# A two-layer attention and feed-forward kernel: the tails of its batches turn their rows on VectorE and through DRAM, and overlap

## The chip, the cores and the metric

The kernel runs on one core of a Trainium2 chip. The core has a matrix engine (TensorE, PE in the profile), VectorE (DVE), ScalarE (ACT), GpSimd (POOL) and SyncE (SP), each with its own instruction queue, and 16 DMA engines. Engines work side by side and wait for each other by semaphores; each runs its own instructions strictly in program order. In this kernel SP does nothing but issue DMAs. The metric is the device time of one execution in microseconds; lower is better. Times before the change are the median of three runs.

## The reference

There are 16 batches (B) of 256 tokens (S) by 256 features (D), in f32. Cut to what matters:

```python
x = x + L0_xattn(ctx, layernorm(x))   # 8 heads of 128; keys from ctx and x together, 512 per query
x = x + L0_ffn(layernorm(x))          # W1, W2 256 x 1024, each plus products of a batch's own tokens; gelu
x = x + L1_xattn(layernorm(x), ctx)   # "second attention": one head of 256, 256 keys
x = x + L1_ffn(layernorm(x))          # 8 experts, routing weights, silu(gate) * up, down
```

## The kernel before

**Layout.** A batch's tokens lie in two chunks (TC = 2) of 128 rows. A matrix product needs the summed index on the partitions, so rows must be turned between stages. Two ways of turning are in use. `transposed` (L269) has TensorE turn four 128x128 blocks into one PSUM bank (`turned`, L87); ScalarE or VectorE then copies it out. A *hop* is the other way: `to_blocks` (L279) lets VectorE turn 32x32 blocks into a tile, and SP writes that to DRAM; `from_blocks` (L293) has SP fetch it back in four DMAs, one for each block row, after which `in_order` only names the pieces in the right order. Hops already turn the inputs of batches 1 to 15, in `inputs`; the first attention's probabilities use the same scheme in `s2` (L820 on).

**Two kinds of work.** The main loop goes over n = 8 * batch + head. A *head step* emits, in this order: `s1(n)` (scores `sc`, row maxima, exponentials), `s1_scale`, `s0q(n+1)` (`pq`), `s0k(n+1)` (`pk`), filling work (`bulk`: `pv`, and units of `inputs`), `s3(n-2)` (`po`, whose result VectorE puts into outT), `s2(n)` (probabilities through DRAM). A place to slip in other work, `gap()`, follows s1, s0q, s0k, each of the two calls of bulk, and s3; I number them 1 to 6. bulk has no `pv` at heads 0 and 1, one at heads 2 to 5 and two at heads 6 and 7. A unit of `inputs(b+1)` comes at heads 0 to 4, in bulk's first call, just after place 3: at head 1 it turns `cin` and `cn` on VectorE and writes them out, at heads 2 and 3 it fetches.

What is slipped in are *chains*, one for each batch. `chain(b)` is a generator which is made at head 2 of batch b+1 and does everything after the first attention: output projection `px` into x, layernorm, turned `ybT`, the batch's own weights (`ev`: two small writes and one 1 MB broadcast read on SP; `od`, `W1e`, `W2e`), `v1`, first feed-forward `ph`, gelu, second `pf`, layernorm `yc`, turned `ycT`, `pq1` (in the trace pq<-ycT,M), scores `sc1`, exponentials `pr`, turned `prT`, `po1` (po<-v,pT), layernorm `row`, turned `ydT`, the routing product `pl`. `route(b)` then works out slots and scatters rows. At the end experts are run over gathered rows, in groups; they fill the same places from the last heads on.

**What sets the order.** Everything is emitted by a planner at build time. `Clock.pe` adds up what TensorE is thought to take: 1.667 ns for a column of f32, at least 0.38 us. A `yield t` in a generator makes it due t us of that clock later. `gap()` runs the first job of `line` that is due until at least 0.8 us of TensorE work has been emitted; older chains stand first. The order that comes out is the program order of all engines' queues. SP's too: a DMA that must wait for its data holds up all DMAs emitted after it.

In a steady batch of the kernel before, chain b starts with px at head 2; y is applied after the last unit of the chain before (`behind.done`), in head 3; ph runs in heads 5 and 6, gelu in head 7 or later, pf up to place 3 of the next batch's head 0, yc at place 1 of head 1, pq1 at place 6, sc1 at place 1 of head 2, po1 at place 4 of head 2, row in head 2, pl at place 3 of head 3.

Of the kernel before, what the change touches and what calls it, by code (L numbers as in the profile page):

```python
# [29 lines left out]
def xattn_ffn_kernel(  # L30
# [37 lines left out]
    def mm_tile(n, name):  # L68
        return psum.tile([P, n], F32, tag="mm", bufs=5, name=name, padded_shape=[P, 512])

    def tr_tile(name):
        return psum.tile([P, 4, P], F32, tag="tr", bufs=1, name=name)

# [191 lines left out]

    def tr_mm_tile(name):
        return mm_tile(4 * P, name).rearrange("p (a t) -> p a t", t=P)

    def transposed(src, name, tile_=tr_tile):  # L269

        t = tile_(name)
        for d in range(DC):
            for c in range(TC):
                turned(t[:, d * TC + c, :], src[:, c, ts(d, P)], ident)
        return t.rearrange("p (d c) t -> p d (c t)", d=DC)
# [47 lines left out]
    def chain(b, A, behind):  # L323
# [8 lines left out]
        def mv_tile(tag):  # L332
            return small.tile([P, TC, 2], F32, tag=f"mv{tag}", bufs=2, name=f"mv_{tag}_{b}")

        mv = mv_tile("b")
        for c in range(TC):
            px = mm_tile(D, f"px_{b}_{c}")
            for h in range(H):
                mm(px, outT[:, h, ts(c, P)], A.Wo[:, h, :], start=(h == 0), stop=(h == H - 1))
                if h == H // 2 - 1:  # L340
                    yield
            nc.vector.tensor_tensor(x_b[:, c, :], px, x_b[:, c, :], ALU.add)
            stats(c, "b", mv)
            if c < TC - 1:
                yield
# [7 lines left out]
        yield 2.5  # L353
        while behind is not None and not behind.done:
            yield 0.4
# [15 lines left out]
        plus_row(x_b, lasting["b2"])  # L371
        yield 2.2
        tp = transposed(y, f"ybT_{b}")
        yT = wk.tile([P, DC, S], F32, tag="yT", name=f"ybT_{b}")
        nc.scalar.copy(yT, tp)
        yield


        v1 = wk.tile([P, TC, D], F32, tag="v1", name=f"v1_{b}")
        for m in range(TC):  # L380
            pv = mm_tile(D, f"pv1_{b}_{m}")
            for d in range(DC):
                mm(pv, cT[:, d, ts(m, P)], WvT[:, d, :], start=(d == 0), stop=(d == DC - 1))
            nc.scalar.copy(v1[:, m, :], pv)
            yield
        yield landed - Clock.pe

        od = wk.tile([P, DC, 2 * NI], F32, tag="od", name=f"od_{b}")
        nc.vector.tensor_scalar(od, yT[:, :, 2 : 2 + 4 * NI : 2], lasting["scale"], None, ALU.mult)
        W1e = wk.tile([P, DC, NI, D], F32, tag="W1e", name=f"W1e_{b}")  # L390
# [29 lines left out]
        for k in range(HC):  # L420
            ph = mm_tile(S, f"ph_{b}_{k}")
            for d in range(DC):
                mm(
                    ph, W1e[:, d].rearrange("p i a -> p (i a)")[:, ts(k, P)], yT[:, d, :],
                    start=(d == 0), stop=(d == DC - 1),
                )
            nc.vector.tensor_scalar(hT[:, k, :], ph, col("b1", k), None, ALU.add)  # L427
            if k % 2 == 1:
                i = k // 2
                if i + 2 < NI:  # L430
                    w1_rows(i + 2)
                if i + 1 < NI:
                    w2_block(i + 1)
                yield 1.0
                w2_add(i)

        done = []
# [13 lines left out]
        for c in range(TC):  # L451
# [7 lines left out]
            if c < TC - 1:  # L459
                yield  # L460


        rs = ln_rstd(mv, "q")
        yield 2.5
        y = wk.tile([P, TC, D], F32, tag="y", name=f"yc_{b}")
        ln_apply(y, x_b, mv, rs)

        plus_row(x_b, lasting["bv1"])
        yield 1.4
        tp = transposed(y, f"ycT_{b}")  # L470
        yT = wk.tile([P, DC, S], F32, tag="yT", name=f"ycT_{b}")
        nc.scalar.copy(yT, tp)
        rc = small.tile([P, TC], F32, tag="rc", bufs=2, name=f"rc_{b}")
        for c in range(TC):
            junk = wk.tile([P, D], F32, tag="pr1", bufs=2, name=f"junk_{b}_{c}")
            nc.vector.tensor_tensor_reduce(
                out=junk, in0=y[:, c, :], in1=g1, op0=ALU.mult, op1=ALU.add,
                scale=1.0, scalar=g0, accum_out=rc[:, c : c + 1],
            )
        yield 1.6  # L480
        q1T = wk.tile([P, DC, S], F32, tag="q1T", name=f"q1T_{b}")
        for m in range(DC):
            pq = mm_tile(S, f"pq1_{b}_{m}")
            for d in range(DC):
                mm(pq, M1[:, d, ts(m, P)], yT[:, d, :], start=(d == 0), stop=(d == DC - 1))
            nc.scalar.activation(q1T[:, m, :], pq, AF.Identity, bias=u1[:, m : m + 1], scale=QS1)
        yield 1.6
        probs = []
        for c in range(TC):
            sc = mm_tile(S, f"sc1_{b}_{c}")  # L490
            for m in range(DC):
                mm(sc, q1T[:, m, ts(c, P)], cT[:, m, :], start=(m == 0), stop=(m == DC - 1))

            nm = small.tile([P, 1], F32, tag="nm1", name=f"nm1_{b}_{c}")
            nc.vector.tensor_reduce(nm, sc, AX.X, ALU.max)
            nc.vector.tensor_tensor(nm, nm, rc[:, c : c + 1], ALU.add)
            nc.vector.tensor_tensor(nm, rc[:, c : c + 1], nm, ALU.subtract)
            pr = wk.tile([P, S], F32, tag="pr1", bufs=2, name=f"pr1_{b}_{c}")
            sm = small.tile([P, 1], F32, tag="sm1", name=f"sm1_{b}_{c}")
            nc.scalar.activation(pr, sc, AF.Exp, bias=nm, accum_out=sm)  # L500
            probs.append((pr, sm))
        yield 3.5
        tp = tr_tile(f"prT1_{b}")
        for c in range(TC):
            for m in range(TC):
                turned(tp[:, c * TC + m, :], probs[c][0][:, ts(m, P)], ident)
        pT = wk.tile([P, TC * TC, P], F32, tag="pT1", bufs=1, name=f"pT1_{b}")
        nc.vector.tensor_copy(pT, tp)
        yield 1.6
        mv = mv_tile("d")  # L510
        for c in range(TC):
            ri = small.tile([P, 1], F32, tag="ri1", name=f"ri1_{b}_{c}")
            nc.vector.reciprocal(ri, probs[c][1])
            po = mm_tile(D, f"po1_{b}_{c}")
            for m in range(TC):
                mm(po, pT[:, c * TC + m, :], v1[:, m, :], start=(m == 0), stop=(m == TC - 1))
            nc.vector.scalar_tensor_tensor(
                x_b[:, c, :], po, ri, x_b[:, c, :], ALU.mult, ALU.add
            )
            stats(c, "d", mv)  # L520
# [9 lines left out]
        nc.vector.tensor_copy(row[:, :, D + E], number[:, b * TC : (b + 1) * TC])  # L530
        yield 1.4
        tp = transposed(row, f"ydT_{b}")
        ydT = wk.tile([P, DC, S], F32, tag="yT", name=f"ydT_{b}")
        nc.scalar.copy(ydT, tp)
        yield 1.6
# [115 lines left out]
    class A:  # L651
        xs, ctxT, outT, cin, kvT, v = {}, {}, {}, {}, {}, {}
        row, z = {}, {}
        projected = set()

# [3 lines left out]
    with ExitStack() as sa, ExitStack() as sf:  # L659
# [18 lines left out]
        def inputs(b):  # L678
# [32 lines left out]
            if b == 0:  # L711
                for src, at_, beta, gamma in ((cn, 0, "bm", "gm"), (xn, S, "bl", "gl")):
                    tp = transposed(src, f"{src.name}_T", tr_mm_tile)
                    for d in range(DC):
                        scaled(tp[:, d, :], d, at_, beta, gamma)
                    yield
                tp = transposed(cin, f"cinT_{b}", tr_mm_tile)
                nc.vector.tensor_copy(A.ctxT[b], tp)
                return
# [117 lines left out]
        def s3(n):  # L837

            b, h = divmod(n, H)
            pT, v = heads.pop(n), A.v[b, h // HG]  # L840
            if h == 0:
                A.outT[b] = wh.tile([P, H, S], F32, tag="outT", name=f"outT_{b}")
            po = mm_tile(S, f"po_{b}_{h}")
            for j in range(JC):
                mm(
                    po, v[:, j, ts(h % HG, DH)],
                    pT.rearrange("p a c f -> p c a f")[:, :, :, ts(j, QB)],
                    start=(j == 0), stop=(j == JC - 1),
                )

            nc.vector.tensor_scalar(A.outT[b][:, h, :], po, col("bv", h), None, ALU.add)  # L851

# [5 lines left out]
        def turn(W, nat, Wt, rchunks, cchunks):  # L858
# [3 lines left out]
            for k in range(0, len(blocks), 4):  # L862
                tp = tr_mm_tile(f"turn_{W.name}_{k}")
                for n, (c, r) in enumerate(blocks[k : k + 4]):
# [11 lines left out]
        def fold(nq, nk):  # L876
# [9 lines left out]
            for d in range(DC):  # L886
                for m in range(DC):
# [3 lines left out]
                    )  # L891
            bkr = wk.tile([P, DC, P], F32, tag="pr1", bufs=2, name="bk_rep")
            for m in range(DC):
# [386 lines left out]
```

## Time and profile before

| | |
|---|---|
| median of three runs | 1898.36 us (1895.84 to 1899.13) |
| the profiled execution's own time | 1899.3 us, span 1897.6 us |
| TensorE busy | 1845.4 us, 97% of the span |
| VectorE, ScalarE, GpSimd busy | 1179.6, 594.8, 872.3 us |
| one batch in the steady part | 93.15 us |
| DMA busy in the steady part | 0.47 of 16 engines |
| mean granted TensorE clock | 0.991 |

A timeline row of the profile gives start and length in us, engine (q: its sequencer, for DMA issues), source line, operation, out<-in, shape and count; what stands in brackets is the idle time before it and what ended it. One f32 product appears as two matmul instructions. A waits row reads: who waited, for what, us in total, times, longest. A row of windows gives the stretch, its length, then busy us (and instructions) of PE, its weight loads, DVE, ACT and POOL, then the granted clock, DMA share and GB/s.

### The profile page before, as it was taken

The numbers are of one execution on the slowest core, as the hardware profiler recorded it, in microseconds if no ns is written. First come the engines' busy times: TensorE is split into PE (matmuls) and PEld (weight loads), VectorE is DVE, ScalarE is ACT, GpSimd is POOL, SyncE is SP. The second block draws the span as 40 slices with busy tenths as digits, with TensorE's granted clock in tenths as the row PEclk, the third lists the DMA queues.
The fourth block names the chain that finished last, engine by engine and source line by source line (L and its number), as shares of the span: only waits on it lengthen the run. The fifth ranks groups of instructions, "written<-read, shape, count | busy, mean of one in ns | idle before, by whom it ended". The sixth has DMA issues, their size and how long they took to land.

```text
span 1897.6 us, 22669 instructions
## 1 busy us (share of the span) xinstructions
PE 1845.4 (97%) x6822; PEld 1252.6 (66%) x6822; DVE 1179.6 (62%) x3211; ACT 594.8 (31%) x1309; POOL 872.3 (46%) x996
## 2 busy tenths in 40 slices
PE   8999999999999999999999999999999999999995
PEld 4566666666666666666666666667676767665554
DVE  5356667666666666666675766666657476656553
ACT  3333434343333333333333333333333221111110
POOL 3122353535353535353534444444434367766565
PEclk9999999999999999999999999999999999999998
DMA  6553445454545444444454444444435477999995
GB/s 217 160 170 103 161 137 159 141 166 138 162 140 159 148 151 157 151 147 149 146 160 151 149 154 143 159 140 160 142 118 177 135 200 194 250 234 241 249 220 96
DMA packets 235083, 309.89 MB, mean 163 GB/s; under 512 B 27036, under 2 KB 195912, under 8 KB 232904
## 3 DMA queue, kind: packets, MB, share of 16 engines
q1 hardware_dynamic: 204184, 256.80, 43.2%
q0 software_dynamic: 30720, 51.54, 11.5%
q8 instruction: 57, 0.93, 0.2%
q14 instruction: 74, 0.61, 0.1%
q10 hardware_dynamic: 48, 0.01, 0.0%
HBM read 157.51 MB, written 150.73 MB: 162 GB/s over the span
## 4 chain that ended last, share of the span: by engine, by line
PE 90%; DVE 3%; DMA 2%; ACT 2%; POOL 1%; issue 1%; SPq 1%; ACTq 0%; POOLq 0%; DVEq 0%
PE po L83 13%; PE pv L83 13%; PE sc L83 12%; PE pk L83 10%; PE pq L83 7%; PE px L83 6%; PE pf L83 6%; PE ph L83 5%; PE pg L83 5%; PE pu L83 5%; PE pd L83 5%; ACT pr L810 1%; DMA wx<-in_L_ffn_Wg_dram 1%; DVE tb L827 1%; POOL out_dram L1123 1%
## 5 line engine op out<-in xcount | busy, mean ns | idle before, releaser
L818 POOL TENSOR_SCALAR pr<-pr,ri 128x512 f32<-128x512 f32 x256 | 183.9, 726 | 478.9 <-DVE ri L817 477.4
L810 ACT ACTIVATE pr<-sc,nm 128x512 f32<-128x512 f32 x256 | 173.8, 683 | 506.2 <-DVE nm L804 505.8
L638 POOL DMA_INDIRECT slots_d<-row,at_slot x256 | 268.7, 1050 | 121.6 <-DVE at_slot L634 64.8
L1123 POOL DMA_INDIRECT out_dram<-o,at x128 | 200.0, 1562 | 128.7 <-DMA out_dram<-o,at 37.8
L83 PE MATMUL po<-pT,v 128*128 128x256 f32 x1024 | 246.9, 385 | 8.9 <-DMA pT<-hop 8.9
L83 PE MATMUL sc<-kT,qT 128*128 128x512 f32 x512 | 241.5, 594 | 0.9 <-ACT kT L743 0.9
L83 PE MATMUL pk<-kvT,Wk_sb 128*128 128x512 f32 x512 | 240.7, 592 | 0.0
L83 PE MATMUL pv<-Wv_sb,kvT 128*128 128x512 f32 x512 | 238.6, 595 | 0.0
L83 PEld LDWEIGHTS po<-pT,v 128*128 128x128 f32 x1024 | 194.2, 192 | 63.2 <-issue 28.4
L804 DVE TENSOR_REDUCE nm<-sc 128x1 f32<-128x512 f32 x256 | 162.1, 666 | 16.9 <-PE sc L83 16.9
L827 DVE STREAM_TRANSPOSE tb<-pr 128x512 f32<-128x512 f32 x256 | 165.3, 683 | 7.2 <-DMA hop<-tb 7.2
L851 DVE TENSOR_SCALAR outT<-po,cvec 128x256 f32<-128x256 f32 x128 | 60.8, 475 | 164.3 <-PE po L83 164.3
L83 PEld LDWEIGHTS pv<-Wv_sb,kvT 128*128 128x128 f32 x512 | 96.0, 190 | 95.1 <-issue 89.2
L83 PEld LDWEIGHTS sc<-kT,qT 128*128 128x128 f32 x512 | 97.5, 191 | 69.4 <-issue 61.5
L83 PEld LDWEIGHTS pk<-kvT,Wk_sb 128*128 128x128 f32 x512 | 97.5, 190 | 68.0 <-issue 61.2
L1098 ACT ACTIVATE sg<-pg 128x384 f32<-128x384 f32 (+3 forms) x82 | 41.3, 504 | 312.3 <-PE pg L83 299.3
L83 PE MATMUL pg<-yTd,wx 128*128 128x384 f32 (+3 forms) x328 | 127.6, 512 | 11.2 <-DMA wx<-in_L_ffn_Wg_dram 7.0
L83 PE MATMUL pq<-kvT,Wq_sb 128*128 128x256 f32 x512 | 132.5, 381 | 0.0
L83 PE MATMUL pu<-yTd,wx 128*128 128x384 f32 (+3 forms) x328 | 125.3, 505 | 0.3 <-DVE hT L427 0.2
L83 PE MATMUL pd<-wx,hTd 128*128 128x256 f32 x512 | 123.8, 379 | 0.2 <-DVE hTd L1109 0.2
L83 PE MATMUL ph<-ybT,W1e 128*128 128x256 f32 x512 | 121.4, 380 | 0.1
L83 PEld LDWEIGHTS pq<-kvT,Wq_sb 128*128 128x128 f32 x512 | 96.6, 191 | 36.7 <-issue 22.7
(197 smaller groups left out, 2685.9 us busy)
## 6 DMA issues: line engine op xcount, KB each, us to landing
hop<-tb SPq DMA_DIRECT2D x128, 512.0 KB
pT<-hop SPq DMA_DIRECT2D x512, 128.0 KB
ev<-ev_d SPq DMA_DIRECT2D x16, 1024.0 KB
rows<-slots_d SPq DMA_DIRECT2D x31, 397.5 KB
hop_rows_b<-rows_b SPq DMA_DIRECT2D x29, 384.0 KB
yTd<-hop_rows_b SPq DMA_DIRECT2D x116, 96.0 KB
rows<-slots_d SPq DMA_DIRECT2D x8, 530.0 KB
cin<-in_ctx_dram SPq DMA_DIRECT2D x16, 256.0 KB
```

Of the source, the lines that this page charges most:

```text
L83: nc.tensor.matmul(out, lhsT, rhs, **kw)
L638: ins = nc.gpsimd.indirect_dma_start(out=slots_d[part], out_offset=bass.IndirectOffsetOnAxis(ap=at_slot[:, c, e : e + 1], axis=0), in_=row ...
L804: nc.vector.tensor_reduce(nm, sc, AX.X, ALU.max, negate=True)
L810: nc.scalar.activation(pr, sc, AF.Exp, bias=nm, accum_out=sm)
L818: nc.gpsimd.tensor_scalar(pr, pr, ri, 1.0, ALU.mult, ALU.mult)
L827: nc.vector.transpose(tb[:, :, c, :], heads[n][c][0].rearrange("p (m f) -> p m f", m=QP))
L851: nc.vector.tensor_scalar(A.outT[b][:, h, :], po, col("bv", h), None, ALU.add)
L1098: nc.scalar.activation(self.sg, self.pg, AF.Tanh, scale=0.5)
L1123: ins = nc.gpsimd.indirect_dma_start(out=out_rows[0 : sum(NTOKS[: self.part + 1]), :], out_offset=bass.IndirectOffsetOnAxis(ap=self.at[:, ...
```

## The change

All four turned tiles of a chain take hops: after each of yb, yc, pr and row, `to_blocks` is emitted at once, `from_blocks` 3.6 us of planner time later, and a use 4.0 later (for yb the 15 us until `ev` is thought to land). yT of the first feed-forward and of pq1 are read in place; pT and ydT are first copied by ScalarE. v1 moves from before ph to between yc's fetch and pq1. The wait for the whole chain in front goes: yb waits until ph of the chain in front is emitted (`fed`), od until its pf is (`fed_forward`), and only yc waits for its end. outT becomes twelve tiles of one head each instead of two of eight heads. PSUM: the bank for turning joins the pool of mm tiles, six instead of five.

```diff
-        return psum.tile([P, n], F32, tag="mm", bufs=5, ...)
-    def tr_tile(name):
-        return psum.tile([P, 4, P], F32, tag="tr", bufs=1, name=name)
+        return psum.tile([P, n], F32, tag="mm", bufs=6, ...)
...
+        def raw_tile(tag, name):
+            return wk.tile([P, QP, DC, TC, QB], F32, tag=tag, name=name)
...
-        while behind is not None and not behind.done:
+        while behind is not None and b - 1 not in A.fed:
             yield 0.4
         y = wk.tile([P, TC, D], F32, tag="y", name=f"yb_{b}")
...
         plus_row(x_b, lasting["b2"])
-        yield 2.2
-        tp = transposed(y, f"ybT_{b}")
-        yT = wk.tile([P, DC, S], F32, tag="yT", name=f"ybT_{b}")
-        nc.scalar.copy(yT, tp)
-        yield
-        v1 = ...   # moved
+        hop = to_blocks(wk, y, TC, "tbc", 1, f"yb_{b}_b")
+        yield 3.6
+        yTb = raw_tile("yT", f"ybT_{b}")
+        from_blocks(yTb, hop)
+        yT = in_order(yTb)
         yield landed - Clock.pe
+        while behind is not None and b - 1 not in A.fed_forward:
+            yield 0.4
...
         rs = ln_rstd(mv, "q")
         yield 2.5
+        while behind is not None and not behind.done:
+            yield 0.4
         y = wk.tile([P, TC, D], F32, tag="y", name=f"yc_{b}")
         ln_apply(y, x_b, mv, rs)
         plus_row(x_b, lasting["bv1"])
-        yield 1.4
-        tp = transposed(y, f"ycT_{b}")
-        yT = wk.tile([P, DC, S], F32, tag="yT", name=f"ycT_{b}")
-        nc.scalar.copy(yT, tp)
+        hop = to_blocks(wk, y, TC, "tbc", 1, f"yc_{b}_b")
...
-        yield 1.6
+        yield 3.6
+        yTc = raw_tile("raw_c", f"ycT_{b}")
+        from_blocks(yTc, hop)
+        landed = Clock.pe + 4.0
+        v1 = ...   # a yield after each of its two products
+        yield landed - Clock.pe
...
-        yield 3.5
-        tp = tr_tile(f"prT1_{b}")
-        for c in range(TC):
-            for m in range(TC):
-                turned(tp[:, c * TC + m, :], probs[c][0][:, ts(m, P)], ident)
-        pT = wk.tile([P, TC * TC, P], F32, tag="pT1", bufs=1, name=f"pT1_{b}")
-        nc.vector.tensor_copy(pT, tp)
+        yield 3.0
+        hop = to_blocks(wk, pr, TC, "tbc", 1, f"pr1_{b}_b")
+        yield 3.6
+        raw = raw_tile("raw_c", f"pr1T_{b}")
+        from_blocks(raw, hop)
+        yield 4.0
+        pT = wk.tile([P, TC, S], F32, tag="pT1", bufs=1, name=f"pT1_{b}")
+        for m in range(TC):
+            nc.scalar.copy(pT[:, m, :], in_order(raw)[:, m])
...
-        yield 1.4
-        tp = transposed(row, f"ydT_{b}")
-        ydT = wk.tile([P, DC, S], F32, tag="yT", name=f"ydT_{b}")
-        nc.scalar.copy(ydT, tp)
+        hop = to_blocks(wk, row, TC, "tbc", 1, f"yd_{b}_b")
+        yield 3.6
+        raw = raw_tile("raw_c", f"ydT_{b}")
+        from_blocks(raw, hop)
+        yield 4.0
+        ydT = wk.tile([P, DC, S], F32, tag="q1T", name=f"ydT_{b}")
+        for d in range(DC):
+            nc.scalar.copy(ydT[:, d, :], in_order(raw)[:, d])
...
-            if h == 0:
-                A.outT[b] = wh.tile([P, H, S], F32, tag="outT", name=f"outT_{b}")
+            o = wh.tile([P, S], F32, tag="outT", bufs=H + H // 2, name=f"outT_{b}_{h}")
+            A.outT.setdefault(b, []).append(o)
```

## The prediction

> **What bounds the kernel now.** I read the page's busy table, then TensorE's waits, then the steady batch from 745.25 to 838.40 us by windows and timelines.
>
> ```profile
> PE 1845.4 (97%) x6822; PEld 1252.6 (66%) x6822; DVE 1179.6 (62%) x3211; ACT 594.8 (31%) x1309; POOL 872.3 (46%) x996
> ```
> ```profile
> PE po L83 <- DMA pT<-hop: 8.9, 2, 4.5
> ...
> PE pl L83 <- ACT ydT L534: 3.4, 14, 0.2
> ```
> ```profile
> 745.25:838.40 93.15, 92.91 (x350) 63.62 (x349) 61.33 (x170) 34.10 (x76) 41.96 (x54) 1.00 0.47 151
> ```
>
> TensorE (first busy figure of the last row) works 92.91 of a batch's 93.15 us. Its only regular wait is pl's, 0.24 us in each of 14 batches. So work taken off TensorE shortens the kernel by its length, and every late operand lengthens it in full: TensorE runs in program order and has nothing to put into a hole.
>
> ```profile
> 745.25 1.88 PE L83 MATMUL sc<-kT,qT 128*128 128x512 f32 x4
> ...
> 749.54 0.60 PE L87 MATMUL ycT<-ident,yc 128*128 128x128 f32 x4
> 749.98 1.89 PE L83 MATMUL po<-pT,v 128*128 128x256 f32 x8
> 751.71 1.89 PE L83 MATMUL pq<-ycT,M 128*128 128x256 f32 x8
> ```
>
> Starts are the honest clock here, since ends are modelled: four turns take 749.98 - 749.54 = 0.44 us, po 1.73, sc and pk 1.71, pq of a head 0.87, a v1 pair 0.86.
>
> **Removed.** 16 batches x 4 groups x 0.436 = 27.9 us of TensorE, and pl's wait, 3.4 us. VectorE gets eight transposes (0.72 for two, the cn row below) and loses pT's copy (0.69): +2.2 us on 61.33 of 93.15, hidden as a sum. ScalarE exchanges three copies of 0.59 for four of 0.40. DMA gets 4 x 512 KB a batch at a share of 0.47, hidden. Six banks for mm, and outT in twelve buffers: nothing, TensorE waits for neither (by my walk head 4 of a batch overwrites head 0 of the last, which px has read two heads earlier). Reading yT in runs of 32 costs nothing: po and pg already read so at full rate.
>
> **Added: four hops, each with five SP issues in program order.** Where they fall follows from the planner's due times. With its 0.43 and 0.85 per 256 or 512 columns I step one batch. The last pf stands after k of head 0, as now, so yc is applied after sc of head 1, as now. Its fetch, due 3.6 later (q + k = 2.56 is short, + po = 4.27), comes after po of head 1, and so behind that head's unit of inputs(), with hop_cin and hop_cn. pq1, due 4.0 later, comes after v1, sc, v1, q (4.27).
>
> ```profile
> 748.56 0.72 DVE L261 TENSOR_SCALAR yc<-x,mv_q,rs_q 128x256 f32<-128x256 f32 x2
> ...
> 754.23 0.72 DVE L285 STREAM_TRANSPOSE cn<-cn 128x256 f32<-128x256 f32 x2
> ```
> ```profile
> 754.98 0.34 SPq L290 DMA_DIRECT2D hop_cn<-cn  x1
> ```
> ```profile
> 774.50 0.33 SPq L831 DMA_DIRECT2D hop<-tb  x1
> 777.16 1.74 SPq L834 DMA_DIRECT2D pT<-hop  x4
> 779.01 1.79 SPq L296 DMA_DIRECT2D raw<-hop_xn  x4
> ...
> 783.29 0.35 SPq L366 DMA_DIRECT2D ev<-ev_d  x1
> 783.73 0.38 SPq L831 DMA_DIRECT2D hop<-tb  x1
> 790.08 1.74 SPq L834 DMA_DIRECT2D pT<-hop  x4
> ```
>
> From these rows: a hop's write lets the next issue go 2.33 us after its own (774.83 to 777.16), or 6.4 us behind ev's 1 MB (783.64 to 790.08); four fetches take 1.8. Landing after the fourth fetch is bounded by two waits of ScalarE in the start-up, 1.67 and 1.89 us, and by raw_xn, issued right behind pT, whose last packet came 2.5 us later. I take 1.8 alone and 2.6 behind pT.
>
> **Wait 1, pq1.** VectorE is busy without a hole from the last pf to cn's transposes, so these end at 754.95 + 0.75 (yc's transposes) - 0.26 (a wait they fill) = 755.44. hop_cn to 755.8, fetches to 757.6, landing 759.4. TensorE is at pq1 at 745.25 + 1.71 + 0.87 + 1.71 + 1.73 + 0.86 + 1.71 + 0.86 + 0.87 = 755.57. It waits 3.8 us (3.7 to 4.6).
>
> **Wait 2, po1.** sc1 comes after k of head 2; pr1's hop, due 3.0, after pv and px; its fetch, due 3.6, misses the last place of head 2 by 0.19 (px + po = 3.41), and so stands behind that head's hop and pT. From the end of po in head 2, SP's path is outT and tb 1.90, hop 0.35 + 2.33, pT 1.74, fetch 1.89, landing 2.6, copy 0.45: 11.3 us. TensorE has px, sc, px, q, k, pv: 9.5 us. It waits 1.8 (1.0 to 2.2).
>
> **Wait 3, pl.** The new chain's yb falls after k of head 3, ahead of row (head 4, after sc). Behind pr1's fetch (8.2 us after that same po) SP has ev_d twice, the wait for it and ev: 2.8, as now from 780.90 to 783.64. yb's hop lands 5.8 behind ev (6.4 less half the hop's data). Then come yb's fetch 1.8, hop and pT of head 3 4.5, row's hop 0.5 + 2.3, fetch 1.8, landing 1.8, copy 0.45: 29.95. TensorE reaches pl after 24.95 + 1.8 of wait 2, and waits 3.2 us. Waits 2 and 3 share one sum, 5.0: if one shrinks the other grows. Behind pl stand pv and ph in TensorE's order; pT of head 3, needed some 3 us later, has landed by 26.
>
> **What a long wait costs besides.**
>
> ```profile
> 1564.43 2.80 PE L83 MATMUL pg<-yTd,wx 128*128 128x384 f32 x4 [2.16 <-DVE o L1122]
> ...
> 1796.68 1.96 PE L83 MATMUL pg<-yTd,wx 128*128 128x512 f32 x4 [1.92 <-DMA wx<-in_L_ffn_Wg_dram]
> ```
>
> After 1.92 us of idleness matmuls ran on at full rate; after 2.16 the smaller pg took 2.80 us for 1.29 of work, and the granted clock stood at 0.5. Start-to-start times give 1.8 us lost after that wait. [...] I go by the row: waits 1 and 3 pay 1.8 each, wait 2 nothing.
>
> **Sum.** Per steady batch 3.8 + 1.8 + 1.8 + 3.2 + 1.8 = 12.4 us; chains 0 to 13 run so: 173.6. Chains 14 and 15 run among the experts, whose rows and fetches share SP; no row prices them. They may gain 5 by starting earlier or lose 25 at 12.4 each; I take +5, nearest to cover, since experts fill more of the distance. The profiled execution's own time is 1899.3 (span 1897.6): 1899.3 - 27.9 - 3.4 + 173.6 + 5 = 2046.6. It lies 0.9 above the median of the runs, so I forecast **2045 us**.
>
> **Rivals.** *One wait only.* Waits 2 and 3 vanish, if SP reaches these fetches earlier than program order by my walk has it (a due time met 0.2 us sooner puts pr1's fetch ahead of pT). Then 14 x (3.8 + 1.8) = 78: 1899.3 - 31.3 + 78 = 1946. For it: the margins of 0.19; against: ev's 1 MB still stands before row's hop.
>
> *Faster: the fetches are in time.* The authors' dues suppose 3.6 us for a hop and 4.0 for a fetch; the rows give 0.7 + 0.35 + 2.3 and 1.8 + 1.8 when neither queue lags. It decides at pq1: if its fetch landed before 755.57, all else covered, the kernel would take 1899.3 - 31.3 = 1868. That asks VectorE to end cn's transposes 3.8 us earlier; its unbroken row of work speaks against it.
>
> *The end grows.* In the experts' stage SP also carries rows, their hops and fetches, and DMA is busy above 0.8 of the time. If each unit of the last two chains waited as long as wait 1, some 15 waits x 3 us give 2090.
>
> *The change doesn't do what it says:* the turns are gone from the program, but the overlap of chains may not matter: each batch starts its chain at head 2 whether or not the last is done; now yb starts 0 to 2 us after pl of the batch before. It moves no time by itself; only its order on SP does, in wait 3.
>
> **Numbers.** Three waits 0.63; one or part 0.19; faster 0.10; the end grows 0.07; the rest 0.01 no change. The likeliest alone is 1995 to 2090: 9.7 to 14.1 us of waits a batch, by the bounds of landing and with one halving of the clock or two, and -5 to +25 for the last chains. The range reaches down through most of the one-wait case: 1935 to 2090. A measurement tells about 0.2% from no change: faster 0.10, same 0.01, slower 0.89.
>
> **What would show it.** TensorE's waits get pq1 <- DMA of yc's fetch (about 3.8 x 14), po1 <- ScalarE's pT copy (1.8) and pl <- ScalarE's ydT copy (3.2); a batch takes about 104 us; granted clock drops twice a batch. SP's timeline shows yc's fetch right behind hop_cn, pr1's behind pT. If a batch takes 91 us and these rows are missing, the walk or VectorE's lag was wrong; if waits stand but the clock stays at 1.0, the clock's term is.

## The result: 2203 us, 16% slower, and the profile after

The changed kernel takes 2203.3 us (median of six runs, 2199.2 to 2214.2) beside 1896.4 us (1888.5 to 1899.1) for the kernel before in the same sessions: a ratio of 1.163, 95% interval 1.159 to 1.166. The forecast was 2045 us with a range of 1935 to 2090. The direction was right; the time lies 113 us outside the range.

The busy table of the changed kernel:

```profile
PE 1939.9 (88%) x6566; PEld 1294.7 (59%) x6566; DVE 1215.0 (55%) x3325; ACT 597.9 (27%) x1323; POOL 863.9 (39%) x996
```

TensorE has 256 instructions fewer, and its busy time went up by 94.5 us: the instructions that are left run longer (295 ns of busy time each, 271 before). The span is 2197.9 us (1897.6 before), and the mean granted clock 0.932 (0.991 before). TensorE's waits of the changed kernel:

```profile
PE pl L80 <- ACT ydT L555: 70.2, 16, 9.8
PE pq L80 <- DMA ycT<-hop_yc_b: 64.6, 16, 5.7
PE pn L80 <- DVE serves L636: 47.2, 15, 3.3
PE po L80 <- ACT pT L525: 18.5, 15, 5.3
```

These four rows come to 200.5 us; before, pl's held 3.4 and pn's 0.5, and the other two were not there. Three of them were forecast; pn waiting for `serves` of the routing was not. The window of one batch, from the start of px to the start of the next px, by the same columns as before:

```profile
769.03:881.63 112.60, 100.41 (x333) 67.10 (x332) 63.61 (x177) 34.40 (x77) 41.33 (x53) 0.92 0.46 143
```

The batch grew from 93.15 to 112.60 us, not to the forecast 104, with TensorE idle for 12.2 us of it and at a clock of 0.92. The timeline of TensorE in that batch shows each wait, and what runs behind it:

```profile
784.99 1.99 PE L80 MATMUL po<-v,pT 128*128 128x256 f32 x8 [1.15 <-ACT pT L525]
...
804.69 1.75 PE L80 MATMUL pl<-Wr_sb,ydT 128*128 128x8 f32 x8 [3.94 <-ACT ydT L555]
806.29 3.76 PE L80 MATMUL pv<-Wv_sb,kvT 128*128 128x512 f32 x4
809.84 2.89 PE L80 MATMUL ph<-ybT,W1e 128*128 128x256 f32 x8
...
825.49 0.61 PE L80 MATMUL pn<-serves,below 128*128 128x16 f32 x2 [3.28 <-DVE serves L636]
...
826.37 3.76 PE L80 MATMUL ph<-ybT,W1e 128*128 128x256 f32 x8
829.92 4.80 PE L80 MATMUL pv<-Wv_sb,kvT 128*128 128x512 f32 x8
...
872.98 3.45 PE L80 MATMUL pq<-ycT,M 128*128 128x256 f32 x8 [3.82 <-DMA ycT<-hop_yc_b]
876.23 2.12 PE L80 MATMUL pk<-kvT,Wk_sb 128*128 128x512 f32 x4
```

The waits add up to 1.15 + 3.94 + 3.28 + 3.82 = 12.19 us. The starts show the slow clock. Behind pl, four pv take 809.84 - 806.29 = 3.55 us, where four take 1.71 in the kernel before; behind pn, eight ph take 3.55 us for 1.73; pq1 takes 3.25 for 1.73. All instructions of the batch summed so, start to start without the waits, take 9.2 us longer than before, which I put down to the clock: some 3.5 after pl, 3.5 after pn, 1.8 after pq1, and small pieces. The sum: 12.2 of waits - 0.2 for pl's wait before + 9.2 of clock - 1.7 of turns = 19.5, by which the batch grew.

Over the whole span the page gives the same picture. New waits less pl's old one: 200.5 - 3.4 = 197. The clock withheld is (1 - 0.932) x 2197.9 = 149 us, against 17 before: 132 more. Less 28 of turns that is 301; the spans differ by 300.3. At the end of pl of chain 13 the changed kernel was already 283 us behind, so the last chains among the experts added only 17.

### The profile page after: what moved, and what is told of

Its sections match the earlier page's. It is cut to its first block, busy times and chain, and to the rows that moved or that the text cites. A ratio compares the mean times of both kernels' runs of the same rounds, so it can differ in the third digit from the quotient of the medians.

```text
span 2197.9 us, 22868 instructions
## 1 busy us (share of the span) xinstructions
PE 1939.9 (88%) x6566; PEld 1294.7 (59%) x6566; DVE 1215.0 (55%) x3325; ACT 597.9 (27%) x1323; POOL 863.9 (39%) x996
## 4 chain that ended last, share of the span: by engine, by line
PE 59%; DVE 16%; DMA 15%; SPq 5%; issue 3%; POOL 1%; ACT 1%; ACTq 0%; DVEq 0%; POOLq 0%
PE pv L80 10%; PE po L80 8%; PE sc L80 5%; PE pk L80 5%; PE pf L80 5%; PE pq L80 5%; PE ph L80 4%; PE pg L80 4%; PE pu L80 4%; PE pd L80 4%; PE px L80 3%; SPq L293 3%; DVE tb L848 3%; DMA hop<-tb 2%; DMA ycT<-hop_yc_b 2%
## 5 line engine op out<-in xcount | busy, mean ns | idle before, releaser
L659 POOL DMA_INDIRECT slots_d<-row,at_slot x256 | 259.4, 1013 | 101.3 <-issue 60.4
L80 PE MATMUL pv<-Wv_sb,kvT 128*128 128x512 f32 x512 | 270.7, 667 | 0.0
L80 PE MATMUL pk<-kvT,Wk_sb 128*128 128x512 f32 x512 | 248.2, 608 | 0.0
L80 PEld LDWEIGHTS pv<-Wv_sb,kvT 128*128 128x128 f32 x512 | 108.8, 216 | 116.4 <-issue 113.3
L80 PE MATMUL ph<-ybT,W1e 128*128 128x256 f32 x512 | 153.9, 454 | 4.4 <-DVE W1e L393 4.4
L80 PEld LDWEIGHTS ph<-ybT,W1e 128*128 128x128 f32 x512 | 119.0, 236 | 46.3 <-issue 21.3
L80 PEld LDWEIGHTS pk<-kvT,Wk_sb 128*128 128x128 f32 x512 | 102.5, 200 | 73.0 <-issue 64.7
```

The source lines that it names most:

```text
L80: nc.tensor.matmul(out, lhsT, rhs, **kw)
L659: ins = nc.gpsimd.indirect_dma_start(out=slots_d[part], out_offset=bass.IndirectOffsetOnAxis(ap=at_slot[:, c, e : e + 1], axis=0), in_=row ...
```

## The experiments

| kernel | median, us | ratio to before, 95% interval | granted clock |
|---|---|---|---|
| changed | 2203.3 | 1.163 (1.159 to 1.166) | 0.932 |
| overlap_alone | 1944.0 | 1.025 (1.022 to 1.029) | 0.984 |
| overlap_pn_later | 1906.1 | 1.005 (1.003 to 1.008) | 0.987 |
| pn_later | 2128.9 | 1.122 (1.118 to 1.126) | 0.945 |
| row_turned | 2061.9 | 1.088 (1.084 to 1.092) | 0.965 |
| row_hop_other_queue | 2161.1 | 1.140 (1.135 to 1.145) | 0.943 |
| filled_waits | 2125.6 | 1.122 (1.117 to 1.127) | 0.981 |
| later_dues | 2043.7 | 1.078 (1.074 to 1.082) | 0.960 |
| ev_other_queue | 2193.8 | 1.157 (1.154 to 1.161) | 0.931 |
| later_dues_ev_other_queue | 2026.5 | 1.070 (1.067 to 1.073) | 0.973 |
| yc_turned (one run) | 2042.9 | | 0.961 |
| yb_hop_alone | 1906.7 | 1.006 (1.004 to 1.008) | 0.990 |
| yb_hop_early_fetch | 1898.8 | 1.001 (1.000 to 1.002) | 0.991 |

### The overlap without any hop: overlap_alone

To the kernel before, the overlap is added, with twelve outT tiles, six mm banks and v1 at its new place. All four turns stay on TensorE.

```diff
-        while behind is not None and not behind.done:
+        while behind is not None and b - 1 not in A.fed:
             yield 0.4
...
+        while behind is not None and b - 1 not in A.fed_forward:
+            yield 0.4
...
+        while behind is not None and not behind.done:
+            yield 0.4
         y = wk.tile([P, TC, D], F32, tag="y", name=f"yc_{b}")
```

> The overlap of the chains, twelve outT buffers and six mm banks alone: all four tiles are turned by TensorE again, with the due times of the kernel before; v1 stays at its new place. Theory (the loss comes with the hops): 1885 to 1905 us, no regular waits of pq1, po1 or pl. Rival (pn's wait, 3.3 us and its clock in 14 batches, belongs to the overlap, since route then shares VectorE with the next chain's ph): 1960 to 1980, with the pn row still there.

It is some 48 us slower than the kernel before, on the side of the rival though not by its amount: the rearrangement costs time without any hop. No run separates the overlap from v1's new place. TensorE's waits of this kernel:

```profile
PE pn L80 <- DVE ri L829: 25.5, 14, 2.2
...
PE pn L80 <- DVE serves L627: 4.4, 2, 3.3
PE ydT L84 <- DVE row L258: 4.2, 1, 4.2
```

In 14 of the 16 chains pn is late by 1.8 to 2.2 us with no hop in the kernel. The new waits less pl's old one are 30.7 us, and the clock takes (1 - 0.984) x 1938.6 = 31 us against 17: together 45, where the two profiled executions lie 41 apart. This is the part of the change that the prediction had put at nothing.

### A later due time for pn: overlap_pn_later and pn_later

One number is changed, once on overlap_alone and once on the changed kernel: the planner places pn 5.0 us behind the routing's VectorE work in place of 1.5.

```diff
         nc.vector.tensor_scalar(flat(rest), flat(wt), 0.0, None, ALU.is_le)
-        yield 1.5
+        yield 5.0
```

> Overlap, twelve outT buffers and six banks without hops, and pn due 5.0 us after its operands are ordered in place of 1.5. Overlap alone took 1944 with pn waiting 1.8 us in 14 batches, half clock behind it. Theory (that wait is the whole cost of the overlap in the steady part): no pn row, a batch of 93.2 us, 1900 to 1915. Rival (the overlap costs elsewhere): 1935 or more.

> The changed kernel with pn due 5.0 us after its operands are ordered instead of 1.5; the four hops stay. Theory (pn's wait is VectorE's lag behind the order, and apart from the hops): the row of 47 us goes and its slow clock, 2 us in 14 batches: 2120 to 2135; pq1, po1 and pl keep theirs. Rival (the time lost at pn is lost anyway at the next operand of VectorE): 2185 or more, with a new wait of ph or po.

Both came out as expected. overlap_pn_later has no pn row, its steady batch is back at 93.26 us with a clock of 1.00, and what is left (9.7 us) lies at the end, where ydT's turn waits 5.2 us for `row` and pg's wait for weights grew from 7.0 to 10.3. pn_later is 74.5 us faster than the changed kernel. Its pn row (47.2) is gone, while pl's grew by 6.5 and a pd row of 5.2 came up; the clock's share fell from 149 to (1 - 0.945) x 2124.3 = 117. So 47 us of wait was worth 74 us of time, the rest by way of the clock.

Why pn is late in the changed kernel shows in VectorE's timeline of it:

```profile
806.95 0.17 DVE L589 SCALAR_TENSOR_TENSOR mask<-z,mask 128x16 f32<-128x16 f32 x1
811.79 0.48 DVE L425 TENSOR_SCALAR hT<-ph,cvec 128x256 f32<-128x256 f32 x1 [4.67 <-PE ph L80]
...
814.90 0.17 DVE L593 TENSOR_TENSOR wt<-wt,mask 128x16 f32<-128x16 f32 x1
...
817.30 0.87 DVE L393 SCALAR_TENSOR_TENSOR W1e<-ev,od,W1T 128x256 f32<-128x256 f32 x2
818.09 1.30 DVE L848 STREAM_TRANSPOSE tb<-pr 128x512 f32<-128x512 f32 x2
...
820.48 0.27 DVE L612 TENSOR_TENSOR ahead<-ahead,same 128x128 f32<-128x128 f32 x1
...
825.27 0.17 DVE L636 TENSOR_SCALAR serves<-wt 128x16 f32<-128x16 f32 x1
```

The routing of one batch (L565 to L636) is a long row of small VectorE operations. In TensorE's timeline of the kernel before, these two rows are 12.6 us apart, and no ph stands between them:

```profile
777.11 1.06 PE L83 MATMUL pl<-Wr_sb,ydT 128*128 128x8 f32 x8 [0.24 <-ACT ydT L534]
...
789.73 0.29 PE L83 MATMUL pn<-serves,below 128*128 128x16 f32 x2
```

In the changed kernel the next chain's ph stands there, and its hT, W1e and W2e stand between the routing's operations in VectorE's one queue. At 807 us the routing is stuck behind an hT that waits for ph, and from 814.5 on VectorE has no hole until `serves`. pn starts 20.8 us after pl.

This meeting of two chains is not what makes pn late in overlap_alone: there ph, hT and W1e come only after pn. VectorE's timeline of overlap_alone, for a chain whose pl starts at 691.68:

```profile
699.24 0.48 DVE L863 TENSOR_SCALAR outT<-po,cvec 128x256 f32<-128x256 f32 x1 [1.61 <-PE po L80]
...
702.48 1.25 DVE L816 TENSOR_REDUCE nm<-sc 128x1 f32<-128x512 f32 x2
...
704.96 0.17 DVE L627 TENSOR_SCALAR serves<-wt 128x16 f32<-128x16 f32 x1
```

The routing's operations now fall at another place of the head step, behind an outT that waits for po and then behind that head's tb and nm. `serves` is done 13.4 us after pl in place of 11.9, while TensorE reaches pn after 11.8 in place of 12.6. In both kernels the planner's 1.5 us between the routing and pn no longer cover VectorE's lag behind the order; with 5.0 us the wait is gone.

### The turn of row back on TensorE: row_turned

```diff
-        hop = to_blocks(wk, row, TC, "tbc", 1, f"yd_{b}_b")
-        yield 3.6
-        raw = raw_tile("raw_c", f"ydT_{b}")
-        from_blocks(raw, hop)
-        yield 4.0
+        yield 1.4
+        tp = transposed(row, f"ydT_{b}")
...
-        for d in range(DC):
-            nc.scalar.copy(ydT[:, d, :], in_order(raw)[:, d])
+        nc.scalar.copy(ydT, tp)
```

> The changed kernel with row's hop alone undone (TensorE turns it, as before). Theory: pl's wait goes, 70 us, and its slow clock, some 30, against 7 us of turns: about 2110. If pn's wait is only a consequence of a late pl, that row (47 us and its clock) goes as well: about 2030. If pn's wait is VectorE's own, in the stretch with ph, the row stays at about 3 us a batch.

It gained 141 us, which lies between the two expected times. TensorE's waits of row_turned:

```profile
PE pq L80 <- DMA ycT<-hop_yc_b: 58.4, 15, 5.6
PE pn L80 <- DVE serves L632: 39.7, 16, 2.7
PE po L80 <- ACT pT L525: 16.8, 15, 5.3
...
PE ydT L84 <- DVE row L258: 7.6, 2, 6.8
PE ph L80 <- PE pk L80: 5.4, 14, 0.4
```

The sum of the changes in these rows is -73 us (pl -70.2, pn -7.5, pq1 -6.2, po1 -1.7, and the last two rows +13.0). The clock gives back 149 - (1 - 0.965) x 2053.7 = 77 us, and the turns cost 7: 143 for the 141 measured. So this one hop, which saves 7 us of TensorE, costs 148 in this kernel, with all that its due times shift. Since pn's wait stays at 2.5 us a chain, most of that wait does not come from row's hop.

### The same hop on another queue: row_hop_other_queue

row's hop and its fetches are issued by GpSimd, where no write of a head and no ev stands ahead of them. The two helpers get a parameter for the queue, not shown here.

```diff
-        hop = to_blocks(wk, row, TC, "tbc", 1, f"yd_{b}_b")
+        hop = to_blocks(wk, row, TC, "tbc", 1, f"yd_{b}_b", queue=nc.gpsimd)
...
-        from_blocks(raw, hop)
+        from_blocks(raw, hop, queue=nc.gpsimd)
```

> The changed kernel with row's hop and its four fetches issued from GpSimd's queue. In its trace row is turned by 793.0 and its hop is issued at 797.55, after the hop and pT of head 3: 4.5 us, as long as pl's wait. Theory (the place behind that round trip on SP makes pl late): pl's row falls from 70 us to under 25, the time with its slow clock to 2090 to 2140. Rival (the round trips of the hop itself, or GpSimd's slower issues, make pl as late): the row stays over 50 us and the time at 2180 or more.

The time fell between the two expectations: 42 us less. pl's row fell from 70.2 to 50.7, just above the rival's 50, and pq1's and pn's stayed. Medians over the first 14 chains show why, all counted from the start of `row`'s application on VectorE:

| | hop issued | first fetch issued | pl starts |
|---|---|---|---|
| changed | 6.8 us | 9.7 us | 13.6 us |
| row_hop_other_queue | 1.8 us | 6.0 us | 12.1 us |
| row_turned | none | none | 3.5 us |

SP's order holds the hop's write back by 5.0 us, yet only 1.5 of that reaches pl, because the hop itself is slower by 3.5 us when GpSimd issues it: 4.2 us from its write to its first fetch where SP's takes 2.9, and 6.1 from there to pl where SP's takes 3.9. So this run does not price the place on SP. The 5.0 us are more than pl's median wait of 4.3 in the changed kernel; that a hop as quick as SP's on a free queue would remove the wait is an estimate from these rows, and no run has it. VectorE and ScalarE are not what holds the hop up once row is there: VectorE has turned row within 1.5 us, and ScalarE's waits of the changed kernel show it standing ready for the fetch in all 16 chains:

```profile
ACT ydT L555 <- DMA ydT<-hop_yd_b: 66.4, 16, 8.3
```

Even with its write sent off at 1.8 us the hop takes 12 us from row to pl, where with the turn pl starts after 3.5 and waits for nothing.

### Work in the holes: filled_waits

Four matmuls of 512 f32 columns, whose result nobody reads, are put ahead of pq1, pl and pn.

```diff
+    def filler(n, name):
+        t = mm_tile(512, name)
+        for _ in range(n):
+            nc.tensor.matmul(t, ident, W1T[:, 0, 0:512], start=True, stop=True)
...
+        filler(4, f"fill_q_{b}")
...
+        filler(4, f"fill_l_{b}")
...
+        filler(4, f"fill_n_{b}")
```

> The changed kernel with four idle f32 matmuls of 512 columns (3.4 us), whose result is never read, put ahead of each of pq1, pl and pn; all else in the same order. They fit into the waits (3.8, 3.9 and 3.3 us). Theory (a good part of the loss, about 9 us a batch, is the clock that is halved after each long wait): granted clock above 0.98 and 2050 to 2110 us. Rival (the clock costs only the 1.8 us twice a batch of the prediction): 2150 to 2170. Rival (the clock costs nothing, the idle time alone is the loss): 2200 or more.

This is above the expected time. The kernel has 384 matmul instructions more, 165 us at 0.43 us each, and is 78 us faster than the changed kernel. pl's wait fell to 22.5, pq1's to 10.3, pn's is gone: 149 us less. The clock rose to 0.981 and so takes 40 us in place of 149. The sum 165 - 149 - 109 = -93 is near the 84 us that lie between the two profiled executions. The holes were filled at no gain of their own, 165 us of work for 149 of waiting; by this sum all the gain is the clock's. It isn't one to use, since it still loses to the kernel before.

### Later due times: later_dues

```diff
-        landed = Clock.pe + 4.0
+        landed = Clock.pe + 8.5
...
-        yield 4.0
+        yield 6.5
         pT = wk.tile([P, TC, S], F32, tag="pT1", bufs=1, name=f"pT1_{b}")
...
-        yield 4.0
+        yield 8.5
         ydT = wk.tile([P, DC, S], F32, tag="q1T", name=f"ydT_{b}")
...
-        yield 1.5
+        yield 5.0
```

> The changed kernel with later due times alone: 8.5 in place of 4.0 us between a fetch and its use for yc and for row, 6.5 for pr, and 5.0 in place of 1.5 ahead of pn. Theory (late operands at four places, and the halved clock after them; no resource is full): the waits of pq1, po1, pl and pn shrink from 200 us in all to under 40, the mean granted clock is back above 0.98, and the time is 1865 to 1920 us. Rival (SP's queue, VectorE or the DMA engines are full, so that operands come as late as before whatever the dues): over 2100 us, with the waits at other places or as long.

It stayed far from the expected time. The four waits nearly went (pl 17.5, pq1 4.0), and a new one came in their place. TensorE's waits of later_dues, first row:

```profile
PE ph L80 <- DVE W1e L393: 62.8, 15, 5.8
```

VectorE's timeline of the same kernel tells what W1e stood behind:

```profile
734.89 1.30 DVE L848 STREAM_TRANSPOSE tb<-pr 128x512 f32<-128x512 f32 x2 [5.20 <-DMA hop<-tb]
...
737.29 0.21 DVE L385 TENSOR_SCALAR od<-ybT,scale_bc 128x16 f32<-128x16 f32 x1
737.54 2.38 DVE L393 SCALAR_TENSOR_TENSOR W1e<-ev,od,W1T 128x256 f32<-128x256 f32 x4
```

tb of the next head overwrites a tile whose hop had not been written yet, since that hop (issued at 731.40) stood on SP behind the fetch of yb (729.56), which stood behind ev (723.22). VectorE was held for 5.2 us, and od and W1e with it.

### ev on another queue: ev_other_queue and later_dues_ev_other_queue

```diff
-        nc.sync.dma_start(ev_d[0:NI, :], y[1 : 2 * NI : 2, 0, :])
-        nc.sync.dma_start(
+        nc.scalar.dma_start(ev_d[0:NI, :], y[1 : 2 * NI : 2, 0, :])
+        nc.scalar.dma_start(
...
-        nc.sync.dma_start(
+        nc.scalar.dma_start(
             ev.rearrange("p n d -> p (n d)"),
```

> The changed kernel with the three DMAs of ev (two small writes and the 1 MB read) issued from ScalarE's queue instead of SP's. Theory (pl is late because SP's order puts ev, the wait for ev_d and the 1 MB ahead of yb's and row's hops): SP loses 2.8 us of issues and the hop of yb lands some 3.6 us earlier behind its own issue, against a sum of 5.0 us of waits at po1 and pl; pl's row falls from 70 us to under 15, and the time by its slow clock too: 2070 to 2120. pn's row stays (about 3 us a batch). Rival (pl is late by VectorE's or the DMA engines' load, not by SP's order): pl's row stays over 50 us and the time within 20 us of 2203.

> Later due times (8.5 after the fetches of yc and row, 6.5 for pr, 5.0 ahead of pn) together with ev's DMAs on ScalarE's queue. With later dues alone one regular wait was left, ph for W1e (62.8 us): VectorE stood 5.2 us at tb, whose buffer SP had not yet written out, behind yb's fetch behind ev. Theory: that row goes, and with it its slow clock: 1890 to 1950. Rival (the wait for W1e is VectorE's own load): the row stays over 40 us, 2020 to 2045.

Neither met its expected time. On the changed kernel moving ev is worth some 10 us, with intervals that overlap, and pl's row hardly moves (65.1): the rival's numbers. They don't rule out SP's order, since row's hop still goes out 6.4 us after the start of row's application (median, 6.8 in the changed kernel). SP's timeline of ev_other_queue:

```profile
786.52 1.25 SPq L852 DMA_DIRECT2D hop<-tb  x1
791.33 1.73 SPq L855 DMA_DIRECT2D pT<-hop  x4
```

yb's hop is no longer behind ev. The head's hop now is the slow one: its issue takes 1.25 us in place of 0.33, and the next issue follows 3.56 us later, where the kernel before shows 2.33. ev had been issued by ScalarE at 783.05; whether that is what slows the hop, no run here separates. On later_dues the same move all but removes ph's wait for W1e (3.9 left), as its theory said, and rows on ScalarE's work take its place: sc waits for kT, 39.3 us, and po1 for its pT, 27.1. The lateness changed its queue, and the kernel gained 17 us where at least 90 were expected, so that its time is the rival's.

### yc's turn back on TensorE: yc_turned

```diff
-        hop = to_blocks(wk, y, TC, "tbc", 1, f"yc_{b}_b")
+        yield 1.4
+        tp = transposed(y, f"ycT_{b}")
+        yTc = wk.tile([P, DC, S], F32, tag="raw_c", name=f"ycT_{b}")
+        nc.scalar.copy(yTc, tp)
...
-        landed = Clock.pe + 4.0
+        landed = Clock.pe + 1.6
```

> The changed kernel with yc's hop alone undone: TensorE turns yc, as before. Theory: pq1's wait (64.6 us) goes, and what follows of slow clock, 1 to 2 us a batch, against 7 us of turns: 2110 to 2150. pl's and pn's rows stay, since SP's order behind them is the same.

The one run took 2042.9 us, well below what was expected. pq1's wait is gone as it should be, but so is po1's, and pl's is down to 6.5; a new row says that sc waits for kT, 54.2 us. An edit of one due time shifts where every later unit of the chain falls, so this run doesn't price yc's hop alone, as row_turned doesn't price row's. The waits that remain still cost: sc's and pn's together 92 us, and 80 of clock.

### One hop on the kernel before: yb_hop_alone and yb_hop_early_fetch

yb's turn alone becomes a hop, without overlap and with twelve outT tiles; the fetch is due 6.0 us later in the first and 3.6 in the second.

```diff
-        yield 2.2
-        tp = transposed(y, f"ybT_{b}")
-        yT = wk.tile([P, DC, S], F32, tag="yT", name=f"ybT_{b}")
-        nc.scalar.copy(yT, tp)
-        yield
+        hop = to_blocks(wk, y, TC, "tbc", 1, f"yb_{b}_b")
+        yield 6.0
+        yTb = wk.tile([P, QP, DC, TC, QB], F32, tag="yT", name=f"ybT_{b}")
+        from_blocks(yTb, hop)
+        yT = in_order(yTb)
```

> The kernel before with yb's hop alone (and outT in twelve buffers, which makes the room): VectorE and DRAM turn yb, its fetch due 6.0 us later, so that it stands behind the same head's hop and pT on SP; no overlap, the other three tiles on TensorE. Theory (a hop pays where its landing is covered; here the 15 us until ev has landed cover it): no new wait, 16 groups of turns less, 7 us: 1888 to 1892. Rival (any further hop holds SP up so that pT comes late): a row po <- pT in every batch, 1900 to 1925.

> The same with the fetch due 3.6 us later, as in the changed kernel, so that it stands ahead of the same head's hop and pT on SP and they wait until yb's hop has landed behind ev's 1 MB. Theory (place on SP decides): pT of that head is issued some 4.2 us later; of its 6.1 us between last issue and use 1.9 are left, against about 2.8 for landing: TensorE waits some 0.9 us a batch, 1900 to 1910, or about 1890 if a landing takes under 1.9. Rival (place does not matter): the same time as the fetch due at 6.0, within 3 us.

Neither is faster than the kernel before, although 7 us of turns are gone, and neither has the rival's row of po waiting for pT in every batch. In yb_hop_alone the loss of 10 us arises largely at one place, the start, in TensorE's timeline:

```profile
145.79 3.78 PE L83 MATMUL ph<-ybT,W1e 128*128 128x256 f32 x8 [4.54 <-DVE W1e L395]
```

The fetch of ybT was issued at 140.80, behind the pT of a head, od came at 144.98, and ph waited 4.5 us and then ran at half rate: the next start comes 3.57 us after its own, at 149.36, where eight ph take 1.73 in the kernel before. From there to chain 13 its batches keep pace with the kernel before, and no more: over twelve batches the four turns give 5.2 us, and the ph take 3.7 more, the sc 1.0, because in some of them TensorE now reaches ph before VectorE has finished W1e. TensorE's timeline of yb_hop_early_fetch has such a row:

```profile
705.57 1.56 PE L83 MATMUL ph<-ybT,W1e 128*128 128x256 f32 x6 [0.21 <-DVE W1e L395]
```

With the earlier fetch the start is mended, and the kernel ties with the one before. But here too the hop arrives late, at VectorE. VectorE's waits of yb_hop_early_fetch have a row that the kernel before has not:

```profile
DVE od L389 <- DMA ybT<-hop_yb_b: 22.9, 15, 5.3
```

In the kernel before, od starts 3.6 us ahead of ph in all the steady batches; with the hop it waits for the fetch and starts only 0.9 to 2.0 us ahead, and W1e, which VectorE makes from od, comes later with it. So the 15 us until ev has landed did not cover this hop. That a hop pays where its landing is covered stays untested: no run here has one.

## Why the prediction failed, step by step

**What bounds it, and direction: right.** TensorE is the bound (97% busy before), late operands count in full (12.2 us of waits in the batch that grew by 19.5), and no other engine's sum of busy time grew much (VectorE's most, by 35.4 us).

**The order on SP and pq1: right.** SP's timeline of the changed kernel, in the same batch:

```profile
785.01 0.34 SPq L368 DMA_DIRECT2D ev<-ev_d  x1
785.46 0.38 SPq L287 DMA_DIRECT2D hop_yb_b<-yb_b  x1
...
791.18 1.73 SPq L293 DMA_DIRECT2D ybT<-hop_yb_b  x4
793.00 0.38 SPq L852 DMA_DIRECT2D hop<-tb  x1
795.72 1.73 SPq L855 DMA_DIRECT2D pT<-hop  x4
797.55 0.38 SPq L287 DMA_DIRECT2D hop_yd_b<-yd_b  x1
800.52 1.73 SPq L293 DMA_DIRECT2D ydT<-hop_yd_b  x4
...
868.15 0.32 SPq L287 DMA_DIRECT2D hop_cn<-cn  x1
868.69 1.82 SPq L293 DMA_DIRECT2D ycT<-hop_yc_b  x4
```

yc's fetch stands right behind hop_cn, yb's hop 0.45 us behind ev, and row's hop behind the head's hop and pT, as walked. The last of row's four fetches is issued 28.0 us after the end of po in head 2 (774.21), where 27.7 was walked. pq1 waits 3.82 us here where 3.8 was worked out, and 53.4 in the first 14 chains where 14 x 3.8 is 53.2. The number owes something to luck: hop_cn went out 0.7 us earlier than walked, and after the last fetch's issue 2.5 us passed where the walk had 1.8.

**po1 and pl: the sum right in this batch, the parts and the total not.** Here 1.15 + 3.94 = 5.1, for 5.0 forecast. Over the kernel the two rows hold 88.7 us, not 70: pl waits 4 to 5.5 us in most chains and 9.8 in one.

**"It moves no time by itself": wrong, and the missing wait.** This sentence of the fourth rival, on the overlap, is the step that failed first. I had put VectorE's growth at "+2.2 us on 61.33 of 93.15, hidden as a sum", and never walked its queue up to pn. overlap_alone shows that the rearrangement costs some 48 us without a hop, and pn_later that pn's wait is worth 74 in the changed kernel. A queue with some 30 us to spare in a batch still came late at one deadline: in the changed kernel because the next chain's feed-forward and the routing met within some 11 us ahead of pn, in overlap_alone because the routing fell behind other work of a head while TensorE came to pn sooner.

**The clock term: right in kind, far too small.** I had 1.8 us after each of two waits, 50 us in 14 batches; one batch loses 9.2 and the kernel 132. The 1.8 came from one wait of 2.16 us. After waits of 3.3 to 3.9 us the loss was 3.5, 3.5 and 1.8, and there are three such waits, not two. The one halving a batch, from which the low end of the likeliest part, 1995 us, is worked out, no run shows for these waits: in the changed kernel's clock records the clock falls to a half two or three times in every steady batch. filled_waits shows the term to be real: 149 us of waiting exchanged for 165 us of work is a gain of 78.

**The end: +5 forecast, 17 measured,** within the bounds given there; the rival of a growing end did not happen.

With three terms the gap is closed, by profiled executions: 2199.6 us against the 2046.6 of the sum, 153 short. pn's 47; the clock's 132 in place of 50; pl, po1 and pq1 at 153 in place of 8.8 x 14 = 123. That is 47 + 82 + 30 = 159, less the 5 that the sum held for the end, since the rows count the last chains too: 154. Of the 13.6 us from row to pl in the changed kernel, the trace gives some 5.3 to the write's place on SP, 1.5 to VectorE and the remaining 6.8 to the hop itself with ScalarE's copy. What stays open is what pl would wait if its hop alone had a queue as quick as SP's, and whether the overlap or v1's new place makes pn late.

## What to carry to other kernels

When chains of work are made to overlap, walk every in-order queue up to each deadline, VectorE's too: a sum with room in it says nothing about one stretch ahead of a deadline (here some 30 us of room in a batch, and pn 3.28 us late). Add to a long TensorE wait the work behind it that runs at half rate: here 197 us of new waits cost 132 us more. Price a transpose that is to leave TensorE by its whole distance (here 13.6 us from row to pl through DRAM, for 3.5 by TensorE), not by the 0.44 us of TensorE that it frees. A due time that is put off can mend a wait, as pn's did in overlap_pn_later, or move the late operand to the next in-order queue, as in later_dues (ph's 62.8 us of waiting for W1e), so look for what now stands behind it.

## What the runs showed of the hardware that I had not expected

**The length of a wait alone did not tell whether half rate followed.** The prediction went by two rows of the kernel before: full rate after 1.92 us, half after 2.16. TensorE's timeline of overlap_alone has the same wait of 1.78 us with either outcome:

```profile
610.62 0.36 PE L80 MATMUL pn<-serves,below 128*128 128x16 f32 x2 [1.78 <-DVE ri L829]
...
611.05 1.96 PE L80 MATMUL pv<-Wv_sb,kvT 128*128 128x512 f32 x4
612.85 1.89 PE L80 MATMUL po<-pT,v 128*128 128x256 f32 x8
...
705.27 0.37 PE L80 MATMUL pn<-serves,below 128*128 128x16 f32 x2 [1.78 <-DVE ri L829]
...
705.71 3.28 PE L80 MATMUL pv<-Wv_sb,kvT 128*128 128x512 f32 x4
708.78 2.31 PE L80 MATMUL po<-pT,v 128*128 128x256 f32 x8
```

Behind the first, four pv take 1.80 us from start to start, and the granted clock is 1.00 from 609.0 to 616.0; behind the second they take 3.07, at a clock of 0.67 from 705.0 to 708.5. In the changed kernel pn waits 3.28 or 3.29 us for `serves` fourteen times. At twelve of these waits a stretch at half clock begins, from 1.06 us before pn starts to 0.31 after; at the two that end at 601.51 and 1731.37 none does, and none at a wait of 2.50 us that ends at 2025.26. At each of the 33 waits of 3.40 us or more that its clock records cover, one begins, within the wait or at most 1.2 us after it.

These records hold 48 stretches at half clock. They begin whole multiples of 3.4133 us apart, to within 0.03, and 45 of them last 3.413 or 6.827 us; that from 805.03 to 811.86 is the one behind the wait of pl shown above. Counted in such steps from the first of the 48, ten of the twelve pn waits begin 0.11 to 1.19 us into a step and two at 3.23 and 3.38; the two without half clock begin at 1.40 and 1.46. That the place of a wait in its step decides is an estimate of mine from these fourteen; no run here moves a wait and nothing else.

**A hop took long even where it did not wait on SP:** 12.1 us from row to pl on GpSimd's queue, for 64 KB in each of four fetches. By the medians of row_hop_other_queue above, 4.2 us pass from the issue of its write to that of its first fetch, and 6.1 from there to pl. In one batch of that run row is applied from 776.26 on and turned by 777.72, 1.5 us later; the write is issued at 778.02 and the first fetch at 782.16.
